# Deformable convolution on one Trainium2 core: transposes into shared PSUM banks, and a longer distance between transpose, copy and product

## The chip, the cores and the metric

The kernel runs on 1 core of one Trainium2 chip. A core has five engines that run side by side, each through its own list of instructions in order: TensorE (PE in the profile, with its weight loads as PEld), VectorE (DVE), ScalarE (ACT), GpSimd (POOL) and SyncE (SP, which only issues transfers here). Sixteen DMA engines move data between HBM and the on-chip memory SBUF. TensorE writes into PSUM, which has eight banks of 2 KB per partition. The metric is the device time of one execution in microseconds (us), median of five runs.

## The reference, cut to what matters

One layer of a vision model on `x` of shape (4, 256, 64, 64) in float32: a normalisation, a deformable 3x3 convolution, an attention over the images of the batch and a mixture of experts. The change lies in the convolution. For each pixel and each of the nine taps the reference predicts an offset and a mask, reads the image at the shifted place by bilinear interpolation (four corners, each with its own weight), and contracts the sampled values with the weights:

```python
off = om[:, :2 * K2].reshape(B, K2, 2, Ho, Wo)
mask = jax.nn.sigmoid(om[:, 2 * K2:])
...
ys = off[:, :, 0] + hs[None, None, :, None] + (ki * DIL)[None, :, None, None]
xs = off[:, :, 1] + ws[None, None, None, :] + (kj * DIL)[None, :, None, None]
sampled = jax.vmap(_bilinear)(x, ys, xs)
sampled = sampled * mask[:, None]
out = jnp.einsum('bckhw,ock->bohw', sampled, w_conv.reshape(O, C, K2))
```

## The kernel before, in words

**Steps.** The convolution is cut into 4 images x 288 = 1152 steps. A step `n` is one tap of one group of 128 pixels (`split`, L740 and on); four steps (`NT`) with the same tap make a block of 512 pixels, and nine taps make a finished block. Each step passes through the engines like this:

- `gather` (L746): POOL issues an indirect DMA that fetches 128 rows of 4 KB (the four corners of 128 pixels) from a table in HBM into one of ten buffers `g`. Gathers are issued in pairs, ten steps ahead, and each waits for the last corner of the step that used its buffer.
- `corner0` (L762): ACT multiplies the first corner by its weight into a tile `s`. It runs `LEAD` = 4 steps ahead.
- `corners` (L779): DVE adds the other three corners with three fused multiply-adds at L774: corner 1 of step n+2 into `partial`, corner 3 of step n+1 into its `s`, corner 2 of step n+2 into its `s`. After corner 3 the sample of a step is complete.
- `turned` (L784): PE transposes the two 128x128 halves of `s` into a PSUM tile `tps` (L788).
- `to_sbuf` (L792): ACT copies `tps` into a quarter of the tile `sT` of this tap (L796), `LAG` = 1 step later.
- `product` (L801): PE multiplies one of the four weight blocks of the tap with `sT`, 128x128 by 128x512, into an accumulator `acc` (L808), `TAP` = 5 steps after the sample. Each step has one such product.

**What else is in the same lists.** After nine taps a block is finished by `ended`: DVE adds the input image (`residual`, L819), PE transposes back and multiplies with the router (`by_token`, L828 and L834), ACT copies out (`done`, L843) and SP stores. Beside this, `pieces` prepares the next image: ACT normalises (L510), PE transposes it for the table (`turn`, L517), ACT copies (`leave`, L530), PE computes the offsets (`rows_of`, L548: six products of 512 columns per block of the image, a block of the image every `PERIOD` = 22 steps), ACT shifts them (L560), PE sums them (`summed`, L569), DVE takes them out (`kept`, L580) and makes positions and weights of them (L620 to L669). For the first image part of this runs during its own steps, and during the last image the first parts of the attention take its place (`first_blocks`).

**What sets the order.** For VectorE, ScalarE, TensorE and GpSimd the order is written out by hand: the loop over `n` calls the functions above in a fixed sequence, and each engine gets its instructions in the sequence of the calls. The waits between engines are put in by the framework from the tiles that are read and written. Two kinds of wait matter below. One is for data: `turned(n)` waits for corner 3 of step n, `to_sbuf` for the transposes, `product` for the copies. The other is for a buffer: `s` has `LEAD + 2` = 6 buffers, `sT` has 2, and the pool `ps_tp` has 3 PSUM banks, which `tps`, the table's transposes (L517) and the transposes back (L828) share.

**After the convolution** comes the attention and the mixture of experts, whose lists stand behind the last step of the convolution on every engine.

Of the kernel before, what the change touches and what calls it, by code (L numbers as in the profile page):

```python
# [9 lines left out]
F32 = mybir.dt.float32  # L10
# [7 lines left out]
P = 128  # L18
B, C, H, W = 4, 256, 64, 64
HW = H * W  # L20
NCH = C // P
K2 = 9
NR = HW // P
NOFF = 3 * K2
QUAD = 32
# [10 lines left out]
BLK = 512  # L36
NT = BLK // P
RB = BLK // W
# [2 lines left out]
STEPS = NR * K2  # L41
NGB = 10
AHEAD = NGB + 1
LEAD, LAG = 4, 1
TAP = LAG + NT
OUT = 6
EARLIEST = 12
FIRST = 32
# [54 lines left out]
def conv_attn_moe_kernel(  # L103
# [140 lines left out]
    state, qks, norms, tps, pending = {}, {}, {}, {}, []  # L244
# [88 lines left out]
    with ExitStack() as actx:  # L333
        aw = actx.enter_context(tc.tile_pool(name="a_w", bufs=1))
        ag = actx.enter_context(tc.tile_pool(name="a_gather", bufs=1))
        asm = actx.enter_context(tc.tile_pool(name="a_sm", bufs=5))
        ast = actx.enter_context(tc.tile_pool(name="a_stage", bufs=1))
        made = actx.enter_context(ExitStack())
        ap_ = actx.enter_context(tc.tile_pool(name="a_params", bufs=2))


        azt = made.enter_context(tc.tile_pool(name="a_zt", bufs=2, side="right"))
        apad = made.enter_context(tc.tile_pool(name="a_pad", bufs=2, side="right"))
        atmp = made.enter_context(tc.tile_pool(name="a_tmp", bufs=1, side="right"))
        axs = [
# [3 lines left out]
        ps_tp = actx.enter_context(tc.tile_pool(name="ps_tp", bufs=3, space=PSUM))  # L349
# [7 lines left out]
        def image_tile(b):  # L357
            xraw[b] = axs[b % 2].tile([P, NCH, HW], F32, name=f"xraw{b}", tag="xraw")
# [11 lines left out]
            load_piece(0, n)  # L370


        woff_sb = aw.tile([P, NCH, 3, 3, QUAD], F32, name="woff_sb")
        V.memset(woff_sb, 0.0)
        for ch in range(NCH):
            nc.sync.dma_start(
# [9 lines left out]
            V.tensor_copy(tap_sum[ps], ident[ps, kj * QUAD : kj * QUAD + NOFF])  # L386


        ocs = [aw.tile([3 * QUAD, RB, W], F32, name=f"oc{n}") for n in range(3)]
        for oc in ocs:  # L390
            V.memset(oc, 0.0)
        wconv_sb = aw.tile([P, NCH, K2, C], F32, name="wconv_sb")
# [2 lines left out]
        rwc_sb = load_router(aw, "rwc_sb")  # L395


        zeros = aw.tile([P, C], F32, name="zeros")
        G.memset(zeros, 0.0)

        def borders(b):
# [11 lines left out]
            )  # L413


        grid = aw.tile([P, 2, NR, K2], F32, name="grid")
        gi = atmp.tile([P, 2, NR, K2], I32, name="gi", tag="ki32")
        for half in range(2):
            ps = slice(half * 64, half * 64 + 64)
# [11 lines left out]
        def pieces(b):  # L431
# [31 lines left out]
            n = FIRST  # L463
# [20 lines left out]
            def block(q, at, table=True, offsets=True, alone=False):  # L484
# [66 lines left out]
                        start=(n == 0), stop=(n == NCH * 3 - 1),  # L551
                    )

                oc = ocs[q % 2 if table else 2]

                def shifted(kj):
                    ps = slice(kj * QUAD, (kj + 1) * QUAD)
# [180 lines left out]
        ss, tps, sTs, accs, sums, backs, outs, last_corner, gathers = ({} for _ in range(9))  # L738

        def split(n):  # L740
            b, m = divmod(n, STEPS)
            j, m = divmod(m, NT * K2)
            k, i = divmod(m, NT)
            return b, j * NT + i, k

        def gather(n):  # L746
            b, r, k = split(n)
            g = G.indirect_dma_start(  # L748
                out=gs[n % NGB], out_offset=None, in_=tables[b],
                in_offset=bass.IndirectOffsetOnAxis(  # L750
                    ap=params[b][0][:, r, k : k + 1], axis=0
                ),
            )


            buffer = f"buffer {n % NGB}"
            tc.declare_no_dep(g.ins, group=buffer, reason="ordered by the last corner")
            tc.add_to_no_dep_group(buffer, g.ins)
            gathers[n] = g
            return g  # L760

        def corner0(n):  # L762
            b, r, k = split(n)
            ss[n] = asm.tile([P, C], F32, name=f"s{n}", tag="s", bufs=LEAD + 2)
            first = S.activation(  # L765
                ss[n], gs[n % NGB][:, :C], AF.Copy, scale=params[b][1][:, 0, r, k : k + 1]
            )
            tc.add_to_no_dep_group(f"buffer {n % NGB}", first.ins)
# [10 lines left out]
        def corners(n):  # L779
            corner(n, 1)  # L780
            corner(n - 1, 3)
            corner(n, 2)

        def turned(n):  # L784
            s = ss.pop(n)
            tps[n] = ps_tp.tile([P, C], F32, name=f"tps{n}", tag="tp")
            for ch in range(NCH):
                T.transpose(  # L788
                    tps[n][:, ch * P : (ch + 1) * P], s[:, ch * P : (ch + 1) * P], ident
                )  # L790

        def to_sbuf(n):  # L792
            tap, i = divmod(n, NT)
            if i == 0:
                sTs[tap] = asm.tile([P, NCH, BLK], F32, name=f"sT{tap}", tag="sT", bufs=2)
            S.copy(  # L796
                sTs[tap][:, :, i * P : (i + 1) * P],
                tps.pop(n).rearrange("p (ch t) -> p ch t", ch=NCH),
            )
# [47 lines left out]
        def ended(block):  # L847

            m = (block * K2 + K2 - 1) * NT + TAP + NCH
            for oh in range(NCH):  # L850
# [14 lines left out]
        def put_off(n, fn):  # L865
            todo.setdefault(n, []).append(fn)
# [87 lines left out]
        with tc.manual_schedule(engines=order):  # L954
            total = B * STEPS
            for n in range(NGB):
                gather(n)
            for n in range(LEAD):
                corner0(n)
            for n in range(2):  # L960
                corners(n)
            for n in range(total + TAP + OUT + 3 * NT):
                b, at = divmod(n, STEPS)
                if at == LOADS[0] and b + 1 < B:
                    image_tile(b + 1)
                    for i, when in enumerate(LOADS):
                        put_off(b * STEPS + when, lambda b=b, i=i: load_later(b, i))
                    for when, fn in pieces(b + 1):
                        put_off(b * STEPS + when, fn)
                if n < total and n % (NT * K2) == 0:  # L970
                    ended(n // (NT * K2))
                if n + LEAD < total:
                    corner0(n + LEAD)
                if n + 1 < total:
                    corners(n + 2)
                if n < total:
                    turned(n)
                if LAG <= n < total + LAG:
                    to_sbuf(n - LAG)
                if 0 <= n - TAP < total:  # L980
                    product(n - TAP)
                if n == (B - 1) * STEPS + EARLIEST:
                    first_blocks()
                for fn in todo.pop(n, ()):
                    fn()

                if n % 2 == 0 and n + NGB < total:
                    g = gather(n + NGB)
                    tc.add_manual_dep(
                        g.ins, last_corner[n + 1].ins.name,  # L990
                        mybir.DependencyInfo(
                            mybir.DependencyClass.Sync, mybir.DependencyReason.DATA
                        ),
                        reason="the next gather's buffer",
                    )
                    gather(n + NGB + 1)
# [10 lines left out]
    for b in range(B):  # L1007
        for j in range(NBLK):
            if j < HB:
                n = j * B + b  # L1010
# [38 lines left out]
    with ExitStack() as bctx:  # L1049
# [4 lines left out]
        ps_tp = bctx.enter_context(tc.tile_pool(name="ps_tpb", bufs=3, space=PSUM))  # L1054
# [76 lines left out]
        total = len(blocks)  # L1131
# [130 lines left out]
    with ExitStack() as bctx:  # L1262
# [6 lines left out]
        ts, os_, pvs, pos_, lns, us, ss, bases = {}, {}, {}, {}, {}, {}, {}, {}  # L1269
# [589 lines left out]
    ps_tp = ctx.enter_context(tc.tile_pool(name="ps_tpm", bufs=2, space=PSUM))  # L1859
# [211 lines left out]
    with tc.manual_schedule(engines={nc.sync.engine, nc.gpsimd.engine}):  # L2071
        fixed.append(True)
        total = len(tiles)
# [79 lines left out]
```

## Time and profile before

| what | value |
|---|---|
| median of 5 runs | 2994.92 us (2992.09 to 3000.05) |
| the profiled execution's own time | 2991.32 us |
| its span in the profile | 2989.5 us |
| mean granted TensorE clock | 0.989 |
| PE busy | 2809.3 us, 94% of the span |
| DVE busy | 2459.3 us, 82% |
| ACT busy | 1897.8 us, 63% |
| POOL busy | 1759.1 us, 59% |
| moved by DMA | 913.00 MB, mean 305 GB/s |
| corners at L774, first and last start | 68.6 us and 1795.1 us |

The span of 2989.5 us is the time from the first to the last instruction that the profile shows; 1.8 us lie around it. The steps of the convolution take from 68.6 to 1795.1 us, 58% of the span, so 1152 steps take 1.50 us each. The page cuts the span into 40 slices of 74.7 us, and the convolution is about slices 2 to 24.

The page is read so: part 1 gives each engine's busy time, part 2 the busy share by slice in tenths, part 5 groups of equal instructions with their count, busy time, mean time of one, and the idle time of the engine just ahead of them with what ended it. A table by windows gives the busy time of each engine in a stretch of time, the granted clock and the DMA rate. A list of waits gives who waited for whom, in total us, times, and the longest.

Busy times of one group can overlap: an engine that works in a pipeline starts the next instruction before the last has ended. So an instruction's cost in a full stretch is the distance between starts, not its duration. In the timeline the products at L808 that follow each other without a break show 12 records in 5.32 us; one `product` of the kernel gives two records, one transpose gives one.

### The profile page before, as it was taken

To read this page: it belongs to the slowest core of one execution; us is meant where nothing else is said; L and a number is where in the kernel's file an instruction comes from. 1 tells how busy PE (TensorE), PEld (TensorE's weight loads), DVE (VectorE), ACT (ScalarE), POOL (GpSimd) and SP (SyncE) were. 2 spreads that over 40 slices of the span, in tenths; PEclk is the share of its full clock that TensorE was granted. 3 is DMA by queue.
4 is the path that set the end of the run, shared out by engine and by line. 5 is a ranking of instruction groups with operands and counts; after the bars stand their busy time and mean duration, and the time that the engine had idled before them with its cause. 6 is when DMAs were issued, how large, how long until landed. Compare 5 with 4: busy or idle time off the path is not lost. (4 is left out here: it accounts for less than half of the span.)

```text
span 2989.5 us, 45522 instructions
## 1 busy us (share of the span) xinstructions
PE 2809.3 (94%) x11356; PEld 1653.7 (55%) x11356; DVE 2459.3 (82%) x6413; ACT 1897.8 (63%) x4462; POOL 1759.1 (59%) x1809
## 2 busy tenths in 40 slices
PE   3899999899998899999999999999999999999997
PEld 2355554345554355544444444455555688888885
DVE  4988889998999999999999996988788785446777
ACT  2566665567765566765766664774876666666665
POOL 2665556666666666666777663320777677774442
PEclk8999999999999999999999999999999999999998
DMA  8999999999999999999999996961555656647988
GB/s 252 399 358 364 348 354 396 406 388 397 407 400 390 398 397 394 399 392 393 398 392 384 384 349 132 182 108 55 185 174 196 187 166 197 206 147 248 340 272 280
DMA packets 348547, 913.00 MB, mean 305 GB/s; under 512 B 42566, under 2 KB 125821, under 8 KB 345984
## 3 DMA queue, kind: packets, MB, share of 16 engines
q0 software_dynamic: 208368, 689.10, 62.5%
q1 hardware_dynamic: 129488, 197.93, 21.3%
q10 hardware_dynamic: 10432, 23.07, 2.0%
q8 instruction: 95, 1.56, 0.2%
q14 instruction: 164, 1.34, 0.1%
HBM read 741.09 MB, written 171.60 MB: 305 GB/s over the span
## 5 line engine op out<-in xcount | busy, mean ns | idle before, releaser
L748 POOL DMA_INDIRECT g<-table,idx x1152 | 1111.6, 965 | 626.8 <-DVE s L774 391.7
L808 PE MATMUL acc<-sT,wconv_sb 128*128 128x512 f32 x2304 | 1189.0, 598 | 29.9 <-ACT sT L796 28.0
L765 ACT ACTIVATE s<-g,wts 128x256 f32<-128x256 f32 x1152 | 586.4, 509 | 393.6 <-DMA g<-table,idx 305.2
L774 DVE SCALAR_TENSOR_TENSOR partial<-g,wts,s 128x256 f32<-128x256 f32 x1152 | 565.5, 491 | 131.6 <-ACT s L765 56.8
L788 PEld LDWEIGHTS tps<-ident,s 128*128 128x128 f32 x2304 | 296.4, 147 | 655.1 <-issue 271.7
L774 DVE SCALAR_TENSOR_TENSOR s<-g,wts,s 128x256 f32<-128x256 f32 x1152 | 551.2, 478 | 0.0
L774 DVE SCALAR_TENSOR_TENSOR s<-g,wts,partial 128x256 f32<-128x256 f32 x1152 | 546.8, 475 | 0.7
L788 PE MATMUL tps<-ident,s 128*128 128x128 f32 x2304 | 458.6, 281 | 85.0 <-DVE s L774 46.5
L796 ACT COPY sT<-tps 128x256 f32<-128x256 f32 x1152 | 414.5, 360 | 145.2 <-PE acc L808 80.9
L1935 POOL DMA_INDIRECT ys_rows<-y,to x277 | 275.1, 993 | 223.8 <-DVE y L1930 167.0
L808 PEld LDWEIGHTS acc<-sT,wconv_sb 128*128 128x128 f32 x2304 | 350.1, 192 | 42.3 <-ACT sT L796 39.3
L1508 POOL DMA_INDIRECT xs_rows<-u,slots x256 | 252.9, 988 | 92.7 <-issue 52.8
L1907 PE MATMUL ph<-xT,w 128*128 128x256 f32 (+1 forms) x1288 | 268.7, 352 | 7.0 <-ACT hT L1911 4.3
L1925 PE MATMUL py<-w,hT 128*128 128x256 f32 x1108 | 266.5, 380 | 0.6 <-ACT w L1874 0.6
L1930 DVE TENSOR_TENSOR y<-py,w 128x512 f32<-128x512 f32 (+1 forms) x161 | 99.4, 617 | 188.4 <-ACT w L1868 75.8
L1907 PEld LDWEIGHTS ph<-xT,w 128*128 128x128 f32 x1288 | 211.3, 191 | 28.0 <-ACT hT L1911 6.7
L1925 PEld LDWEIGHTS py<-w,hT 128*128 128x128 f32 x1108 | 207.4, 191 | 26.9 <-ACT w L1874 1.0
L1911 ACT ACTIVATE hT<-ph,w 128x256 f32<-128x256 f32 (+1 forms) x322 | 136.2, 442 | 128.2 <-PE ph L1907 126.5
L322 DVE SCALAR_TENSOR_TENSOR junk<-q,k 128x512 f32<-128x512 f32 x224 | 141.5, 687 | 20.4 <-ACT k L1107 20.3
L548 PE MATMUL po<-xs,woff_sb 128*96 128x512 f32 x288 | 147.3, 593 | 0.0
L1290 DVE SCALAR_TENSOR_TENSOR mix<-pv,att,mix 128x512 f32<-128x512 f32 x192 | 132.7, 743 | 6.8 <-PE pv L1026 2.8
L1874 ACT COPY w<-early_state 128x768 f32 x161 | 132.9, 825 | 0.0
(291 smaller groups left out, 3436.1 us busy)
## 6 DMA issues: line engine op xcount, KB each, us to landing
xt<-xs_rows SPq DMA_DIRECT2D x116, 260.0 KB
yk<-ys_rows SPq DMA_DIRECT2D x56, 512.0 KB
table<-zt SPq DMA_DIRECT2D x96, 256.0 KB
g<-table,idx POOLq DMA_INDIRECT x1152
t<-o SPq DMA_DIRECT2D x32, 530.0 KB
t<-bo_sb POOLq DMA_DIRECT2D x32, 530.0 KB
dt<-t SPq DMA_DIRECT2D x64, 265.0 KB
xraw<-in_x SPq DMA_DIRECT2D x16, 1024.0 KB
```

The source lines that it names most:

```text
L322: V.scalar_tensor_tensor(junk, qks[s_, j, ch][0], 1.0, qks[t_, j, ch][1], ALU.mult, ALU.mult, accum_out=parts[:, ch, s_ * B + t_, j : j + 1],)
L548: T.matmul(t["po"], woff_sb[:, ch, ki].rearrange("p kj o -> p (kj o)"), t["xs"][:, ch, ki : ki + RB], start=(n == 0), stop=(n == NCH * 3 - 1),
L748: g = G.indirect_dma_start(out=gs[n % NGB], out_offset=None, in_=tables[b], in_offset=bass.IndirectOffsetOnAxis(ap=params[b][0][:, r, k : ...
L765: first = S.activation(ss[n], gs[n % NGB][:, :C], AF.Copy, scale=params[b][1][:, 0, r, k : k + 1])
L774: last_corner[n] = V.scalar_tensor_tensor(kept if c == 1 else ss[n], gs[n % NGB][:, c * C : (c + 1) * C], params[b][1][:, c, r, k : k + 1] ...
L788: T.transpose(tps[n][:, ch * P : (ch + 1) * P], s[:, ch * P : (ch + 1) * P], ident)
L796: S.copy(sTs[tap][:, :, i * P : (i + 1) * P], tps.pop(n).rearrange("p (ch t) -> p ch t", ch=NCH),)
L808: T.matmul(accs[block, oh], wconv_sb[:, ch, k, oh * P : (oh + 1) * P], sTs[tap][:, ch, :], start=(k == 0 and ch == 0), stop=(k == K2 - 1 a ...
L1508: s = G.indirect_dma_start(out=rows_, out_offset=bass.IndirectOffsetOnAxis(ap=slots[:, k, n : n + 1], axis=0), in_=u[:, n % NT, :], in_off ...
L1907: T.matmul(ph, w1_sb[:, ch, f * P : (f + 1) * P], xT[:, ch, :], start=(ch == 0), stop=(ch == NCH - 1),)
L1925: T.matmul(py[:, i, :], hT[:, f, i * P : (i + 1) * P], w2_sb[:, f, :], start=(f == 0), stop=(f == NCH - 1),)
L1935: s = G.indirect_dma_start(out=ys_rows[g], out_offset=bass.IndirectOffsetOnAxis(ap=to[:, i : i + 1], axis=0), in_=y[:, i, :], in_offset=No ...
```

## The change

Four things change in the convolution.

1. **Pairs in PSUM.** `turned` makes a tile of two steps (2 KB per partition, a full bank) at every even step, and the odd step writes the second half. The pool still has 3 banks.
2. **Distances.** PE transposes step n-1 instead of n (`TURN` = 1), ACT copies step n-3 instead of n-1 (`LAG` = 3), and the product stands 9 steps behind the sample instead of 5 (`TAP` = `LAG + NT + 2`). All that hangs on `TAP` (adding the input, transposing back, storing) moves 4 steps later with it.
3. **More buffers.** `s` gets `LEAD + TURN + 2` = 7 instead of 6, `sT` 3 instead of 2.
4. **Room for them.** The offset weights, the grid, the zeros and the tiles `oc` move into a pool that is given back when the last table has been made, and `oc` has two tiles instead of three: one for the tables of later images instead of two in turn, one for the first image.

The number of instructions of each kind and engine stays the same, but for one memset of `oc` less on DVE. Behind the convolution the lists of PE, ACT and DVE are the same in both kernels. On SP a store of a finished block changes places with a border store once, and with two weight loads once; on POOL one memset moves ahead of some constants.

```diff
-LEAD, LAG = 4, 1
-TAP = LAG + NT
+LEAD, TURN, LAG = 4, 1, 3
+TAP = LAG + NT + 2
...
+        amade = made.enter_context(tc.tile_pool(name="a_made", bufs=1, side="right"))
...
-        woff_sb = aw.tile([P, NCH, 3, 3, QUAD], F32, name="woff_sb")
+        woff_sb = amade.tile([P, NCH, 3, 3, QUAD], F32, name="woff_sb")
...
-        ocs = [aw.tile([3 * QUAD, RB, W], F32, name=f"oc{n}") for n in range(3)]
+        ocs = [amade.tile([3 * QUAD, RB, W], F32, name=f"oc{n}") for n in range(2)]
...
-                oc = ocs[q % 2 if table else 2]
+                oc = ocs[0 if table else 1]
...
-            ss[n] = asm.tile([P, C], F32, name=f"s{n}", tag="s", bufs=LEAD + 2)
+            ss[n] = asm.tile([P, C], F32, name=f"s{n}", tag="s", bufs=LEAD + TURN + 2)
...
         def turned(n):
             s = ss.pop(n)
-            tps[n] = ps_tp.tile([P, C], F32, name=f"tps{n}", tag="tp")
+            if n % 2 == 0:
+                pair = ps_tp.tile([P, 2, C], F32, name=f"tps{n}", tag="tp")
+                tps.update({n: pair[:, 0, :], n + 1: pair[:, 1, :]})
             for ch in range(NCH):
                 T.transpose(
                     tps[n][:, ch * P : (ch + 1) * P], s[:, ch * P : (ch + 1) * P], ident
...
-                sTs[tap] = asm.tile([P, NCH, BLK], F32, name=f"sT{tap}", tag="sT", bufs=2)
+                sTs[tap] = asm.tile([P, NCH, BLK], F32, name=f"sT{tap}", tag="sT", bufs=3)
...
-                if n < total:
-                    turned(n)
+                if TURN <= n < total + TURN:
+                    turned(n - TURN)
                 if LAG <= n < total + LAG:
                     to_sbuf(n - LAG)
                 if 0 <= n - TAP < total:
                     product(n - TAP)
```

More of the change, by code (lines that the diff above doesn't have):

```diff
@@ L395, in conv_attn_moe_kernel @@
         rwc_sb = load_router(aw, "rwc_sb")
-        zeros = aw.tile([P, C], F32, name="zeros")
+        zeros = amade.tile([P, C], F32, name="zeros")
         G.memset(zeros, 0.0)
@@ L413, in borders @@
             )
-        grid = aw.tile([P, 2, NR, K2], F32, name="grid")
+        grid = amade.tile([P, 2, NR, K2], F32, name="grid")
         gi = atmp.tile([P, 2, NR, K2], I32, name="gi", tag="ki32")
```

## The prediction

> **What bounds the kernel now.** First the busy shares by slice on the page, to find the stage and its engines:
>
> ```profile
> PE   3899999899998899999999999999999999999997
> ...
> DVE  4988889998999999999999996988788785446777
> ACT  2566665567765566765766664774876666666665
> ...
> DMA  8999999999999999999999996961555656647988
> ```
>
> In the slices of the convolution (2 to 24) PE, DVE and DMA all stand at 8 or 9 and ACT at 6: the slices alone don't say who sets the pace. So I asked for the table by windows of 100 us from 80 to 1780 us (PE, PEld, DVE, ACT, POOL busy, then clock, DMA share, GB/s):
>
> ```profile
> 280.00:380.00 100.00, 98.62 (x380) 51.12 (x379) 82.43 (x216) 66.68 (x161) 56.20 (x61) 1.00 0.98 358
> ...
> 680.00:780.00 100.00, 100.00 (x411) 54.33 (x410) 89.54 (x212) 71.70 (x176) 64.44 (x70) 1.00 1.02 399
> 780.00:880.00 100.00, 100.00 (x414) 54.58 (x414) 91.65 (x228) 69.96 (x175) 64.59 (x70) 1.00 1.03 403
> 880.00:980.00 100.00, 90.52 (x329) 42.53 (x328) 91.90 (x216) 55.11 (x146) 65.28 (x70) 0.97 1.01 393
> 980.00:1080.00 100.00, 89.06 (x322) 40.63 (x322) 96.36 (x239) 58.40 (x148) 65.60 (x68) 1.00 1.01 392
> ```
>
> The stage has two kinds of stretch. Where the next image's table and offsets are made (180 to 480, 680 to 880, 1080 to 1280: the seven P windows) PE is full: its seven busy times are 98.46, 98.62, 97.15, 100, 100, 99.06 and 99.78, so it idles 6.9 us in 700. In the other ten, the D windows, PE has 4 to 13 us free in each and DVE sets the pace. DVE's idle there is 62.3 us in 1000, but most is not waiting. In the timeline corner 1 starts 0.57 us after corner 2, which took 0.48, with no releaser named: a fixed distance that the change does not touch:
>
> ```profile
> 1791.82 0.47 DVE L774 SCALAR_TENSOR_TENSOR s<-g,wts,partial 128x256 f32<-128x256 f32 x1
> 1792.39 0.49 DVE L774 SCALAR_TENSOR_TENSOR partial<-g,wts,s 128x256 f32<-128x256 f32 x1
> ```
>
> So I asked for the waits of DVE alone. In the D windows they are 3.1 us (80 to 180), 3.8 (480 to 680), 3.5 (880 to 1080), 5.4 (1280 to 1480) and 1.2 (1480 to 1780): 17.0 us in all. In one of these windows, 880 to 1080, the waits of all engines show what is behind them:
>
> ```profile
> ACT s L765 <- DMA g<-table,idx: 56.2, 79, 2.7
> ...
> ACT sT L796 <- PE acc L808: 6.1, 9, 1.4
> ...
> DVE partial L774 <- ACT s L765: 3.5, 8, 0.8
> ```
>
> The reader is to see that DVE waits for corner 0, and that ACT, which makes it, is mostly held by gathers, little by PE.
>
> **What this says of the ceiling.** The page shows large waits, but a wait counts only on the engine that is full in its stretch. DVE waits 55 us in the P windows (21.9 us of it on PE's sums at L569), yet PE could not have gone faster there by more than 6.9 us. PE waits for DVE's corner 3 in the D windows, where DVE is the bound. If every wait on the full engine went, the stage would gain 6.9 + 17.0 = 23.9 us of 2991.
>
> **The change part by part.**
>
> *Transposes one step behind.* `turned` no longer needs the corner 3 that DVE has just finished. In the P windows this is PE's wait of 2.5 us (180 to 480, L788 on DVE s; none is shown in the other four P windows). It goes. PE may also enter each P stretch up to one step ahead. A step's PE work is two transposes and a product; in the timeline transposes to product is 0.22 us and a product 0.86 (the 12 records between 1796.10 and 1801.25 us are six products), so 1.08. Three P stretches give 0 to 3.2 us; PE is held by ACT's copies as well as by DVE, so I take 2.
>
> *Products four steps further behind, third `sT`.* The wait of products for copies (L808 on ACT sT, 2.1 us in 180 to 480) goes; with the 2.5 that is 4.6 of the 6.9 us, and I take 4.6 (bounds 0 and 6.9). ACT's wait for a free `sT` (L796 on PE acc, 80.9 us on the whole page) should nearly vanish, since the third buffer gives it three steps of room instead of one. ACT is 60 to 70% busy, so this pays only where it made corner 0 late. I went back from each of the 17.0 us in the D windows to what had held ACT: about 9 us end at a gather that had not landed, which the change cannot hurry. Bounds 0 and 17.0; I take 7, nearer to 17.0 - 9.
>
> *Pairs.* The transposes of a step, their copies and their PSUM space cost the same instructions as before. Two waits are new. The copy of an even step now waits for the odd step's transposes too, as they share a bank; behind it on ACT stands the next corner 0, and DVE waits for that. The copies stand one step behind those transposes, as every copy did before, when a copy started 1.3 us (P) to 1.8 us (D) after its transposes in the middle case: hidden. And the waits written into the built program show that the transposes of an even step, where a table is made, wait for the copy of three steps before, which stands one step earlier on ACT (elsewhere five steps before); the table's transposes take turns in the same three banks. Before, every step waited for the copy of two or three steps before, also one step earlier on ACT. So half of these waits go and the other half keeps its distance. I take 0 for it; the rival below prices it.
>
> *The tail.* After the last corner 3, PE has nine products to go instead of six, and the attention's list stands behind them on PE. Three more products cost 3 x 0.86 = 2.6 us:
>
> ```profile
> 1795.88 0.38 PE L788 MATMUL tps<-ident,s 128*128 128x128 f32 x2
> 1796.10 5.32 PE L808 MATMUL acc<-sT,wconv_sb 128*128 128x512 f32 x12
> 1801.25 0.27 PE L828 MATMUL back<-ident,sum 128*128 128x128 f32 x1
> ```
>
> PE is at 100% soon behind it (1816 to 1846 us), so this is on the path. At the start the later products cost nothing: PE is 88% busy from 80 to 180 us.
>
> *Moved tiles, one `oc`, order on SP.* One `oc` for the tables is written again 17 steps (25 us) after its last sums; if that cover were gone, a wait like DVE's longest on L569, 3.4 us, could come once per block. A store that changes places with two weight loads on SP is read no sooner than before; 0, at worst one landing of some 8 us as for the stores at the end of the chain. The memset of `oc` that goes (0.54 us) lies before the first image has landed: 0.
>
> **A rule that speaks against it.** The rate of DMA in the windows above goes up to 403 GB/s, in a slice of the page to 407, at a share of 1.0. The Trainium skill (DMA: Bandwidth & Descriptors, Where 436 GB/s comes from) says that about 358 GB/s binds for transfers between HBM and SBUF and 435 GB/s is the ceiling of the fabric. The first figure would make any gain here impossible; the rows already stand above it. By the second, an estimate, the stage's 390 GB/s would leave some 10%, more than the change can use. Likewise the skill (PSUM — Partial Sum Buffer, PSUM bank collisions raise a hardware error) asks that two engines be kept apart by bank, not by address, which agrees with the wait of the even copy on the odd transposes; no row of before shows such a pair.
>
> **Sum.** 4.6 + 2 + 7 - 2.6 = 11.0 us less. The profiled execution took 2991.3 us (span 2989.5 and 1.8 around it), so 2980.3 on its own scale. It lies 3.6 us under the median of the five, 2994.9; on the median's scale the forecast is 2983.9, taken as 2984.
>
> **Rivals.**
>
> *Nothing is left (0.27).* All 17.0 us of the D windows turn out to be the gathers', and the P windows gain 4.6 at most: 4.6 - 2.6 = 2 us, 2993. For it: 56.2 us against 6.1 in the waits of ACT above, and a DMA share of 1.0.
>
> *Larger (0.15).* PE's busy time is modelled, so a window of 98% may hide stalls. If half of DVE's 55 us of waits in the P windows also go with the new room: 11 + 27 = 38 us, or with only a third 29; I price it at 2960. Against it: the starts of products there keep to 0.43 us a record.
>
> *Slower (0.13).* In the P windows PE is full, so any new wait on it shows in the time. The place is the transposes of even steps, held by the copy three steps before, which in turn stands behind corner 0 and its gather on ACT. 700 us at 1.50 us a step are 467 steps, 233 pairs. In 680 to 880 us PE's weight loads waited on such copies 24 times for 6.5 us, 0.27 each, all hidden behind the matmul before. If a third of the pairs wait that long in the open: 78 x 0.27 = 21, and the tail 2.6: 24 us, 3018. It decides from the point where ACT's copy ends after PE has finished the product before it; in the P windows the copy of two steps before ended 1.5 us ahead of the transposes in the middle case, and after them in 7 cases of 100, so ACT would have to lose about a step.
>
> **Numbers.** 0.45 for the forecast (2977 to 2989), 0.27 for nothing left, 0.15 for larger, 0.13 for slower. About 0.2%, 6 us, is what a measurement of this kernel can tell from no change, so faster is 0.45 + 0.15 = 0.60, same 0.27, slower 0.13. The range reaches from 2962 (all 23.9 us, the 3.2 of the lead, and some of the larger case) to 3002 (nothing left and the lower part of the slower case).
>
> **What would show it.** Right: in the P windows PE stays at 98 to 100% and the windows only get shorter by 1%; ACT's wait at L796 for acc falls from 80.9 us to under 20; the D windows' waits of DVE fall from 17 to about 10, all behind gathers; nine products at the end. Wrong: PE's share falling under 97% in the P windows with the transposes (L791 there) waiting for copies (slower), or DVE's om waits gone and PE showing more work per us (larger).

## The result, and the profile after

The changed kernel takes **2999.81 us** (median, 2993.51 to 3006.11). The kernel before, run beside it, takes 2993.85: ratio 1.0019, 95% interval [1.0014, 1.0024]. The interval lies wholly above 1, so it is slower, by about the 0.2% (6 us) that the prediction took for the least that can be told; the forecast was 2984 and faster. The span of the profiled execution is 2994.4 us against 2989.5, at the same mean clock of 0.989. Beside the runs e9 to e18 the kernel before itself took 3336 to 3379 us, at a mean clock of 0.94; those runs are compared only with each other.

The busy shares by slice of the changed kernel:

```profile
PE   4899998899998899998999999999999999999997
...
DVE  4988889998998998999999996887788785445777
ACT  2566765566665566655676664665876666666675
...
DMA  8999999999999999999999996961555656657988
```

PE, DVE and DMA stand at 8 or 9 in the convolution as they did, and nothing in this view tells the kernels apart. The table by windows (PE, PEld, DVE, ACT, POOL busy with counts, then clock, DMA share, GB/s):

```profile
280.00:380.00 100.00, 100.00 (x395) 52.97 (x393) 82.35 (x219) 67.16 (x163) 56.35 (x61) 1.00 0.96 354
680.00:780.00 100.00, 98.91 (x405) 53.55 (x404) 88.82 (x211) 68.30 (x170) 64.28 (x68) 1.00 1.02 394
780.00:880.00 100.00, 100.00 (x407) 53.84 (x406) 92.08 (x228) 69.27 (x175) 64.68 (x69) 1.00 1.02 399
880.00:980.00 100.00, 88.93 (x334) 41.49 (x333) 89.91 (x213) 55.00 (x146) 65.21 (x69) 1.00 1.01 394
980.00:1080.00 100.00, 86.59 (x325) 41.21 (x325) 96.01 (x238) 58.51 (x150) 66.70 (x67) 1.00 1.01 390
```

The reader is to look at the counts. From 680 to 880 us PE is still "full" at 98.91 and 100.00, but it starts 405 + 407 matmul records there, before 411 + 414. A record of a product lasts 0.59 us while the next starts after 0.43, so busy time says "full" well before the engine is. In 280 to 380 us, in image 0, the count rises from 380 to 395. A single window also shifts with where its edges cut the steps, so the table by groups of steps further down is the safer measure. The waits from 880 to 1080 us:

```profile
ACT s L766 <- DMA g<-table,idx: 55.1, 85, 2.4
...
PE tps L791 <- ACT sT L799: 15.1, 19, 1.8
DVE partial L775 <- ACT s L766: 6.3, 16, 1.1
```

ACT's wait for products (6.1 us before) has gone from the list; its wait for gathers has not moved (56.2 to 55.1), and DVE waits longer for corner 0 (3.5 to 6.3), not less. The end of the convolution, DVE's last corners and then PE:

```profile
1795.97 0.47 DVE L775 SCALAR_TENSOR_TENSOR s<-g,wts,partial 128x256 f32<-128x256 f32 x1
1796.53 0.49 DVE L775 SCALAR_TENSOR_TENSOR partial<-g,wts,s 128x256 f32<-128x256 f32 x1
```

```profile
1798.66 0.38 PE L791 MATMUL tps<-ident,s 128*128 128x128 f32 x2
1798.88 7.89 PE L811 MATMUL acc<-sT,wconv_sb 128*128 128x512 f32 x18
1806.61 0.27 PE L831 MATMUL back<-ident,sum 128*128 128x128 f32 x1
```

The corners keep their distance of 0.56 us, and 18 records, nine products, take 7.89 us where 12 took 5.32. From the last corner 1 to the start of the last record it is 9.7 us, before 7.1: 2.6 us of tail. The rest of the loss is in the steps, and small: the last corner 1 starts at 1796.5 instead of 1793.7.

**Where the waits of ACT went.** ACT's waits from 68 to 1796 us, before:

```profile
ACT s L765 <- DMA g<-table,idx: 305.2, 457, 14.3
ACT sT L796 <- PE acc L808: 80.9, 123, 2.9
ACT sT L796 <- PE tps L788: 60.3, 113, 1.6
ACT s L765 <- DVE s L774: 52.6, 85, 2.5
...
ACT zt L530 <- PE tpx L517: 37.9, 59, 1.6
```

and after:

```profile
ACT s L766 <- DMA g<-table,idx: 318.1, 467, 13.1
ACT zt L531 <- PE tpx L518: 85.5, 68, 2.8
ACT s L766 <- DVE s L775: 67.7, 99, 3.0
...
ACT sT L799 <- PE tps L791: 35.4, 64, 2.0
ACT s L766 <- DVE partial L775: 26.1, 44, 2.1
ACT s L766 <- PE tps L791: 24.7, 42, 1.5
```

The 80.9 us are gone and 25 us of the wait for transposes with them. The same time comes back in front of the next instruction that can't go on: the table's transposes (37.9 to 85.5), gathers (305.2 to 318.1), buffers `s` (52.6 to 67.7, and 24.7 for transposes that still read them, which the list of before does not have). All of ACT's waits in this stretch together are 620 us before and 637 after. DVE's wait for corner 0 over all steps is 56.8 and 57.5 us.

**A new wait.** With the products `residual` moves four steps back, and the load of the next image's first quarter writes the buffer that `residual` reads. SP's waits from 68 to 1796 us, first before, then after:

```profile
SPq L363 <- DVE s L774: 221.3, 12, 35.4
```

```profile
SPq L364 <- DVE s L775: 133.2, 10, 19.6
...
SPq L364 <- DVE sum L822: 70.3, 2, 35.3
```

Twelve loads waited only for their place in the order; now two of them, the first of images 2 and 3, wait for the sum of the block before and start at step 10.1 of the image instead of 6.7. DVE's statistics of the image then wait for data that had always been there (1.1 us in all).

Time by groups of steps, from the starts of corner 1, in us (D: no table is made, P: a table is made):

| steps | before | changed | e2 | e5 | e6 | e7 | e8 |
|---|---|---|---|---|---|---|---|
| 0-60, D | 97.5 | 97.4 | 96.8 | 95.9 | 96.2 | 96.8 | 96.7 |
| 60-250, P, image 0 | 307.4 | 305.8 | 307.4 | 307.4 | 305.8 | 279.2 | 279.3 |
| 250-348, D | 146.5 | 148.3 | 146.2 | 144.1 | 144.5 | 146.5 | 149.1 |
| 348-538, P, image 1 | 277.6 | 279.0 | 279.0 | 277.1 | 274.2 | 274.5 | 274.9 |
| 538-636, D | 147.3 | 148.7 | 146.1 | 143.9 | 144.1 | 147.8 | 148.2 |
| 636-826, P, image 2 | 282.8 | 282.8 | 283.1 | 280.7 | 277.7 | 277.5 | 278.2 |
| 826-924, D | 138.7 | 138.9 | 137.3 | 136.6 | 136.8 | 138.3 | 138.1 |
| 924-1151, D | 327.5 | 327.0 | 326.6 | 327.1 | 327.0 | 328.9 | 327.0 |

e2 is before with the third `sT` alone, e5 and e6 are before and changed with gathers of half the size, e7 and e8 before and changed with five of six offset products left out. Each column is one execution, so a single cell is worth a microsecond or two; the P group of image 0 repeats better than that (307.4 in before, e2 and e5, 305.8 in the changed kernel and e6).

DVE's own waits in the D groups behind step 60, added up in the same way, say more than the windows of 100 us, which cut into P groups: 11.0 us before, 14.4 in the changed kernel, 7.4 in e2, 0.9 in e5 and 2.2 in e6.

### The profile page after: what moved, and what is told of

Same layout as the page of the kernel before. It is cut to its first block, busy times and chain, and to the rows that moved or that the text cites. A ratio compares the mean times of both kernels' runs of the same rounds, so it can differ in the third digit from the quotient of the medians.

```text
span 2994.4 us, 45056 instructions
## 1 busy us (share of the span) xinstructions
PE 2805.6 (94%) x11356; PEld 1655.5 (55%) x11356; DVE 2459.3 (82%) x6412; ACT 1884.7 (63%) x4462; POOL 1761.1 (59%) x1809
## 5 line engine op out<-in xcount | busy, mean ns | idle before, releaser
L766 ACT ACTIVATE s<-g,wts 128x256 f32<-128x256 f32 x1152 | 586.0, 509 | 454.4 <-DMA g<-table,idx 318.1
L775 DVE SCALAR_TENSOR_TENSOR partial<-g,wts,s 128x256 f32<-128x256 f32 x1152 | 565.6, 491 | 131.1 <-ACT s L766 57.5
L799 ACT COPY sT<-tps 128x256 f32<-128x256 f32 x1152 | 411.2, 357 | 39.2 <-PE tps L791 37.7
L549 PE MATMUL po<-xs,woff_sb 128*96 128x512 f32 x288 | 147.3, 593 | 0.0
```

Source lines behind the costliest of these rows:

```text
L549: T.matmul(t["po"], woff_sb[:, ch, ki].rearrange("p kj o -> p (kj o)"), t["xs"][:, ch, ki : ki + RB], start=(n == 0), stop=(n == NCH * 3 - 1),
L766: first = S.activation(ss[n], gs[n % NGB][:, :C], AF.Copy, scale=params[b][1][:, 0, r, k : k + 1])
L775: last_corner[n] = V.scalar_tensor_tensor(kept if c == 1 else ss[n], gs[n % NGB][:, c * C : (c + 1) * C], params[b][1][:, c, r, k : k + 1] ...
L799: S.copy(sTs[tap][:, :, i * P : (i + 1) * P], tps.pop(n).rearrange("p (ch t) -> p ch t", ch=NCH),)
```

## The experiments

**First, the terms of the prediction one by one.** My theory after the result: three limits, PE, DVE and the gathers, lie so close that room on one of them is taken up by the next; the tail and the late load then decide. Rival: the new layout itself costs waits (pairs in three banks, copies behind corner 0) that cancel a real gain.

*e1: the changed kernel with a product two steps nearer.*

```diff
-TAP = LAG + NT + 2
+TAP = LAG + NT
```

> The changed kernel with the product 7 steps behind the sample instead of 9, all else as changed. Theory A (the full engine of each stretch sets the time; the change only moved waits and lengthened the tail): seven products instead of nine behind the last transposes, 2 x 0.86 = 1.7 us less than the changed kernel, about 1.0013 of before. Rival B (the room between copies and products is worth something): slower than the changed kernel, above 1.0019. Rival C (shared PUSM banks of the pairs hold PE): no difference to the changed kernel, 1.0019.

3000.4 us, ratio 1.0023, [1.0010, 1.0035]. The tail is 8.4 us (9.7 in the changed kernel, 7.1 before), so 1.2 of the expected 1.7 us came back at the end, but not in the time, which can't be told from the changed kernel's 1.0019: the two later P groups took 280.8 and 284.7 us, 1.8 and 1.9 more than in the changed kernel. PE's waits from 68 to 1803 us show what the shorter distance costs inside:

```profile
PE acc L811 <- ACT sT L799: 73.9, 69, 3.5
```

In the changed kernel no wait of a product for a copy is in the list, and before they came to 28.0 us. PE stops 25 times for over 1.5 us during the steps of e1 (7 times in the changed kernel, 5 before), and the granted clock is 0.50 for 37.5 us of them (3.4 in the changed kernel). So the two steps of room between copy and product do remove waits of PE; what that is worth in time can't be told here.

*e2: the third `sT` alone.* Distances and single tiles as before, with the moved pool.

```diff
-LEAD, TURN, LAG = 4, 1, 3
-TAP = LAG + NT + 2
+LEAD, TURN, LAG = 4, 0, 1
+TAP = LAG + NT
```

> The distances and single PSUM tiles of before, with the changed kernel's pool layout and three sT buffers: of the change, only the third sT and the moved tiles are left. Theory A: the wait of copies for a free sT (80.9 us on ACT) falls under 20, and the time stays within 3 us of before (0.999 to 1.001). Rival B (ACT's waits for PE made corner 0 late and so cost time): 6 us or more faster, below 0.998. If the new layout itself costs something, it shows here as above 1.001.

2992.17 us, 0.9996 [0.9987, 1.0006]: no change. ACT's waits from 68 to 1796 us:

```profile
ACT s L766 <- DMA g<-table,idx: 291.5, 469, 2.9
ACT sT L797 <- PE tps L789: 106.3, 169, 2.0
```

The wait of 80.9 us for a free `sT` is gone, and 46 us of it stand one line further, at the transposes (60.3 before). This is the cheapest form of what happened to the whole change: most of ACT's wait moved on by one line. It is not all of it. DVE's waits in the D groups behind step 60 fall from 11.0 to 7.4 us, and these groups are 3.7 us shorter together, while the P groups are 1.7 longer. All steps together are 2.7 us shorter in this one execution, and the medians' 2.1 us lie inside the interval of no change.

*e3: the copies of the table and of the finished blocks later on ACT* (changed kernel), so that they no longer hold it up.

```diff
-                        out_.append((at + 4 + 4 * i, lambda i=i: leave(i)))
+                        out_.append((at + 6 + 4 * i, lambda i=i: leave(i)))
...
-                put_off(m + OUT + 2 * i + 1, lambda i=i: done(block, i))
+                put_off(m + OUT + 2 * i + 2, lambda i=i: done(block, i))
```

> The changed kernel, with the copies of the table's transposes two steps later (three behind them instead of one) and those of the transposes back one step later. Theory A: ACT's waits there (85.5 and 58.7 us in the changed kernel) fall under 60 together, and the time falls by 0 to 5 us against the changed kernel (1.0003 to 1.0019 of before), as PE is full where tables are made. Rival B (these two waits took the place of the ones removed and ate a gain of some 14 us): 10 us or more faster than the changed kernel, below 0.9985 of before.

3007.59 us, 1.0040 [1.0027, 1.0053], some 6 to 8 us worse than the changed kernel, which neither theory had foreseen. ACT's two waits leave its list, but its wait for transposes at L799 rises from 35.4 to 128.0 us. PE's waits from 68 to 1803 us:

```profile
...
PE tps L791 <- ACT sT L799: 38.0, 57, 1.7
PE acc L811 <- DVE sum L822: 13.6, 27, 0.9
PE back L831 <- ACT o L846: 11.7, 15, 2.1
PE back L831 <- ACT sT L799: 11.6, 12, 1.7
```

A later copy holds its bank of the pool of three longer, and PE waits for banks at the transposes back: `back` on copies of `o`, 11.7 us, is not among PE's waits of the changed kernel. That this is what costs the time is argued: a fourth bank would test it, and the convolution's pools take all eight (3 + 1 + 2 + 2).

*e4: the kernel before with the table's work spread wider.*

```diff
-PERIOD = 22
+PERIOD = 25
-BORDERS = 236
+BORDERS = 257
```

> The kernel before with one block of the next image's table every 25 steps instead of 22 (and the borders' store at step 257 instead of 236): the same work on PE spread over more steps, no distance or buffer changed. Theory A (PE is full where tables are made, and DVE elsewhere): a period's PE work of 22 x 1.535 = 33.8 us takes 37.5 us with three more steps of 1.25, where before it took 33.8 and three steps of 1.475, 38.2; 0.7 us for 24 blocks, about 17 us, at least 8: 0.994 to 0.997 of before. Rival B (short waits between the engines cost the time, not a full PE): no gain, 0.999 or above.

2993.43 us, 0.9998 [0.9990, 1.0007]. The P groups got shorter (277.6 to 273.8, 282.8 to 275.5 us) and the D groups behind them longer (147.3 to 153.0, 138.7 to 143.6). So 8 us or more for a PE that is full, as theory A had it, did not come. The run doesn't settle it alone: the first gathers of images 1 and 2 start 2.8 and 6.2 us late (0.5 before), probably behind the later store of the borders.

**Then one limit taken away at a time.**

*e5 and e6: half the bytes of each gather,* on the kernel before and on the changed one. The right-hand corners are not fetched and count as zeros or old values; two of the ten buffers are cleared first.

```diff
-                out=gs[n % NGB], out_offset=None, in_=tables[b],
+                out=gs[n % NGB][:, : 2 * C], out_offset=None, in_=tables[b],
```

> The kernel before with gathers of 2 KB a row instead of 4: the two right-hand corners are not fetched, DVE still adds what stands in the buffers. Every instruction of PE, DVE and ACT stays. Theory A (PE full where tables are made, DVE elsewhere, gathers hold the rest): DVE's waits behind gathers go, and what is left is the full engines: 10 to 30 us faster, 0.990 to 0.997. Theory D (the gathers' rate sets the time over each image, so that what one stretch gains another loses): 25 us or more faster, below 0.992. Rival B (short waits between PE and ACT): under 6 us, above 0.998.

> The changed kernel with the same half gathers. Theory A: the change still buys nothing, 0 to 6 us slower than the kernel before with half gathers (the tail of 2.6 us and what moved waits cost). Theory D: with the gathers out of the way the new room pays: 6 us or more faster than the kernel before with half gathers.

Before: 2979.37 us, 0.9948 [0.9934, 0.9962]. Changed: 2976.98, 0.9935 [0.9921, 0.9948]. ACT's waits in e5, 68 to 1796 us:

```profile
ACT sT L798 <- PE acc L810: 254.7, 251, 3.6
ACT sT L798 <- PE tps L790: 186.9, 327, 2.0
...
ACT s L767 <- DMA g<-table,idx: 29.2, 38, 3.1
```

and in e6:

```profile
ACT s L768 <- DMA g<-table,idx: 148.2, 209, 4.0
```

With lighter gathers ACT's waits on them fall from 305.2 to 29.2 us. In the table by steps the D groups up to 924 lose 9.5 us (the sum of 1.6, 2.4, 3.4 and 2.1): that is close to the "about 9 us that end at a gather" of the prediction, and DVE's waits in the D groups behind step 60 all but go (11.0 to 0.9). The P group of image 0 stays at 307.4 us, so there the gathers hold nothing. And now the change pays where it was meant to: e6 is 2.9 and 3.0 us faster than e5 in the P groups of images 1 and 2, and 1.6 in that of image 0. With full gathers those two groups gained -1.4 and 0.0. Over all steps it is 6.4 us faster in e6 than in e5, in the medians 2.4: the tail of 2.6 us stays, and in the trace the steps of e6 start 1.0 us later. The two intervals overlap, and 2.4 us faster is neither the 0 to 6 us slower of theory A nor the 6 us or more of theory D, so the sum is weaker evidence than its place.

*e7 and e8: five of six offset products left out,* on both kernels, so that PE has far less to do in the P groups. Offsets and addresses come out different.

```diff
-                        start=(n == 0), stop=(n == NCH * 3 - 1),
+                        start=True, stop=True,
...
-                    for m in range(NCH * 3):
+                    for m in range(1):
```

> The kernel before with one of the six products that make the offsets of a block, five left out (160 products of 0.86 us, so PE has some 130 us less to do, nearly all where tables are made; offsets and addresses are other ones). Theory A: the P windows take the step of the D windows, 1.475 instead of 1.535 us: 27 us faster, at least 15, 0.988 to 0.995. Theory D: the gathers hold the P stretches as well; under 12 us, above 0.996.

> The changed kernel with the same five of six offset products left out. Theory A: no better than the kernel before with them left out, 0 to 6 us slower. Rival B (the new room pays where PE is not full): 6 us or more faster than it.

Before: 2959.87 us, 0.9881 [0.9866, 0.9896]; changed: 2963.24, 0.9896 [0.9880, 0.9911]. The windows of e7, behind the first of them in the kernel before:

```profile
180.00:280.00 100.00, 98.46 (x403) 53.21 (x402) 83.61 (x223) 70.46 (x168) 57.70 (x61) 1.00 0.96 353
...
180.00:280.00 100.00, 93.85 (x395) 50.27 (x394) 94.28 (x248) 74.55 (x182) 66.04 (x70) 1.00 1.03 401
680.00:780.00 100.00, 93.16 (x374) 49.07 (x374) 90.46 (x216) 70.53 (x175) 66.74 (x70) 0.98 1.03 409
```

In image 0 the P group falls from 307.4 to 279.2 us: there PE was the limit (DMA moved 353 GB/s in that window before, 401 now). In images 1 and 2 the same relief gives 3.1 and 5.3 us of 280, though PE drops to 93% busy. So behind PE, at 1 to 2%, stands another limit; the gathers, at a DMA share of 1.03, fit it best after e6, and DVE, 90% busy, may have a part. "PE is full, hence PE sets the pace" was true for one P stretch in three. The time meets theory A's range at its edge (0.9881), but 28 of the 36 us come from image 0, not from all P groups. The other offsets also send the gathers to other rows of the table; what that alone does wasn't tried. With PE off the path the change costs 3.4 us in the medians (in the traces 2.6 of tail and 2.2 in the steps).

**Then the parts, to find which one loses the 2.8 us in the steps.** e9 loads the images and starts their pieces four steps later; e10 has the transposes a step behind, without pairs; e11 the pairs, without that; both with copies two steps behind and the product six. e12 is e4 with a smaller spread.

```diff
 e9, on the changed kernel
-FIRST = 32
-LOADS = (8, 18, 28, 38)
+FIRST = 36
+LOADS = (12, 22, 32, 42)
 e10, on the changed kernel, with single tiles in turned
-LEAD, TURN, LAG = 4, 1, 3
-TAP = LAG + NT + 2
+LEAD, TURN, LAG = 4, 1, 2
+TAP = LAG + NT
 e11, on the changed kernel
-LEAD, TURN, LAG = 4, 1, 3
-TAP = LAG + NT + 2
+LEAD, TURN, LAG = 4, 0, 2
+TAP = LAG + NT
 e12, on the kernel before
-PERIOD = 22
+PERIOD = 24
-BORDERS = 236
+BORDERS = 242
```

> The changed kernel with the next image's four loads 4 steps later (steps 12, 22, 32, 42 instead of 8, 18, 28, 38) and what follows them in step (FIRST 36 instead of 32). Theory E (the change moved the last use of the image's buffer behind the step of the first load, so the load comes 3.4 steps late and crowds the next one and the gathers): DVE's wait for the image (1.1 us) goes and the two stretches around the image's start shorten by 2 to 4 us together: 1.0004 to 1.0014 of before. Rival: the late load costs nothing, 1.0019 as the changed kernel.

> Of the change only the transposes one step later (TURN 1, copies at 2, products at 6, so copy and product keep their distances to the transposes), with three sT and seven s; single PSUM tiles as before. Six products behind the last transposes as before, so no longer tail, and the image's buffer is free in time. Theory A: no room that the full engine can use, 0.9993 to 1.0007. Rival B (DVE's corner 3 held PE): 6 us or more faster, below 0.998.

> Of the change only the pairs in PSUM (transposes in their own step, copies at 2, products at 6), with three sT. One product more behind the last transposes, 0.9 us. Theory C (pairs and the table's transposes take turns in three banks, and PE waits for copies): 2 to 8 us slower than before, 1.0007 to 1.0027, with PE's wait for copies above the 17 us of before. Without C: 1.0003.

> The kernel before with a block of the next image's table every 24 steps and the borders' store at step 242, right behind the last table store. With 25 steps and the borders at 257 the two P stretches of images 1 and 2 were 3.8 and 7.3 us shorter, and the first gathers of images 1 and 2 waited 2.8 and 6.2 us. If those waits were the late borders': 2 to 8 us faster than before, 0.9973 to 0.9993. If the gathers' rate takes back what PE gains (theory D): 0.9995 to 1.0005.

The kernel before took 3379.05 us beside these four. e9 3366.68, 0.9967 [0.9949, 0.9985]; e10 3357.62, 0.9939 [0.9917, 0.9961]; e11 3351.5, 0.992 [0.9891, 0.9949]; e12 3378.68, 0.9998 [0.9975, 1.0022]. Parts of a change that gains nothing now gain 0.3 to 0.8%. So the parts were run again, with the changed kernel itself beside them:

> The changed kernel with the image loads and the first piece of each image four steps later, so that no load waits for an addition that has not been made. The time before here is near 2995 if the chip grants its full clock. If the late load is what costs the 1.8 and 1.4 us of the steps 250 to 348 and 538 to 636: 3.2 us less than the changed kernel, ratio about 1.0008. If that cost comes from the longer room itself (another order of waits on ACT): within 1 us of the changed kernel, 1.0015 to 1.0020.

> Transposes one step behind, copies one step behind those, product at the old six-product distance plus one, single tiles instead of pairs. If the transposes' step is what gains and the pairs lose: 0.9975 to 0.999. If there is nothing to gain because table, gathers and VectorE limit within 1 to 2 per cent of each other: 0.9995 to 1.0015, the tail costing at most 1.7 us.

> Pairs in PSUM with the transposes at their old place, copies two steps behind, one step more for the product. If pairs relieve PE of waits for copies: 0.997 to 0.999. If pairs in three banks cost waits: 1.001 to 1.003. If nothing is left to gain: 0.9995 to 1.0015.

> The changed kernel itself, on the same chip as the other three, as the point they are compared with. At full clock 1.0019 as before. On a chip that grants a lower clock, where PE is the longer engine: 0.992 to 0.998, as its parts did there.

Before 3375.12; e13 (as e9) 3369.72, 0.9982 [0.9962, 1.0003]; e14 (as e10) 3354.56, 0.9933 [0.9908, 0.9959]; e15 (as e11) 3350.65, 0.9926 [0.9899, 0.9952]; e16, the changed kernel, 3352.59, 0.9926 [0.9899, 0.9952]. And a third time for two of them:

> The changed kernel with image loads and first pieces four steps later, a third try to see it where the clock is full (before near 2995). There: 1.0008 if the late load costs the 3.2 us by which the steps 250 to 348 and 538 to 636 are longer, 1.0015 to 1.0020 if it doesn't. Where the clock is 0.94 (before near 3375): 0.997 to 0.998 as in the two runs before, which says that starting the pieces later costs more there than the load's wait.

> Pairs with the transposes at their old place, copies two steps behind, seven products at the end. At full clock: 0.9990 to 1.0000 if the step's delay of the transposes and the longer tail are what made the changed kernel slower, 1.001 to 1.003 if the pairs themselves cost. At a clock of 0.94: 0.992 to 0.993 as before.

Before 3336.07; e17 3316.66, 0.9935 [0.9914, 0.9956]; e18 3311.85, 0.9923 [0.9897, 0.9950].

The changed kernel, 0.2% slower than a kernel before of 2994 us, is 0.7% (22.5 us) faster than one of 3375. The chip alone does not make that difference: on the one of e17 and e18 the kernel before took 2995.56 us beside e5 to e8. What the parts were to show, where the 2.8 us of the steps go at 2994, none of these runs shows. Of the expectations for the lower clock, those of e16 and e18 came in, and e17's (0.997 to 0.998) did not. A trace shows what these executions have besides a lower clock. ACT's row of instructions in e16:

```profile
522.51 0.36 ACT L799 COPY sT<-tps 128x256 f32<-128x256 f32 x1
529.79 0.38 ACT L846 COPY o<-back 128x265 f32<-128x265 f32 x1 [6.92 <-remote]
530.07 0.51 ACT L766 ACTIVATE s<-g,wts 128x256 f32<-128x256 f32 x1
```

and the windows just behind it:

```profile
530.00:532.00 2.00, 1.78 (x9) 1.78 (x10) 1.30 (x4) 1.90 (x7) 0.00 (x0) 0.50 0.95 383
532.00:534.00 2.00, 2.00 (x5) 0.86 (x5) 1.91 (x5) 1.32 (x4) 0.88 (x1) 0.50 0.66 269
```

ACT stands still for 6.92 us, with "remote" as the releaser, which is none that the trace can name; the product of PE that it copies had ended at 522.3. PE and DVE run dry behind it, and when PE returns its clock is 0.50 for some five microseconds. From 80 to 1950 us there are 43 PE gaps over 1.5 us in e16 and 50 in e12, which has the old distances; the trace of the kernel before at 2991 us has 5. Why the change gains among such stops is not shown: turn alone, pairs alone and the whole change agree within their intervals. What the three share is the third `sT`, copies at least a step further behind and a later product. Starting the pieces later takes some of the gain away again beside e16 (e13, the intervals lie apart), but not beside e18 (e17).

## Why the prediction was wrong

- **The tail, +2.6 us: right**, to the tenth (7.1 to 9.7 us). Behind it the rest of the kernel takes 1188.3 us in the changed trace and 1188.7 before, so nothing absorbed it.
- **Transposes and products in the P windows, -4.6 and -2: failed.** The step was "In the P windows PE is full, so a PE wait removed is time". The P groups together went from 867.8 to 867.6 us. In image 0 PE is the limit (e7: 28.2 us) and 1.6 us came. In images 1 and 2 the gathers are a limit as well: with full gathers the change brings -1.4 and 0.0 us there, and a gain of 2.9 and 3.0 only when they are halved (e5 to e6), one execution each. I had read a busy share of 100 as a limit on its own, with a DMA share of 1.02 to 1.03 in the same rows.
- **DVE's waits in the D windows, -7: failed.** They went from 17.0 to 20.4 us. The step was to take what is left of 17.0 beside the 9 us of the gathers as the missing `sT` buffer's. In the D groups themselves, behind step 60, DVE waits only 11.0 us, and with half gathers 0.9 are left (e5): nearly all of it is the gathers'. ACT's 80.9 us at `acc` did fall to 0, as forecast, and turned up in front of other instructions (e2 shows it for the buffer alone: 60.3 to 106.3 us at the transposes, time 0.9996). The buffer alone may be worth half of the 7 (e2: 7.4 us of waits, D groups 3.7 us shorter); with the distances, the pairs and the late load on top these waits are 14.4, so those three together put 7.0 us back. These are sums over one execution each, and they overlap: a late corner 0 can have both a gather and a buffer behind it. Which of the three costs what is open.
- **The step that was not in the sum: `residual` moves with `TAP`.** I costed the later products only at the start and the end. The first image load now waits for it; the D groups 250 to 348 and 538 to 636 are 1.8 and 1.4 us longer, 1.5 and 1.9 in e3, and -0.3 and -1.2 in e2, where the load is in its old place. The D group 826 to 924, which has no load, is 0.3 us longer in the changed kernel and as before in e3. That the load is the cause is still argued: DVE's direct wait for it is only 1.1 us; the same late load goes with 0.4 and 0.2 us under halved gathers (e6 against e5) and with 2.6 and 0.4 under less PE work (e8 against e7); in e1, where it starts 1.4 steps late instead of 3.4, the two groups are 3.1 and 1.2 us longer, but many of that run's PE stops lie in them; and e9, e13 and e17, which were to show it, ran beside a kernel before of 3336 to 3379 us.
- **The rivals.** "Nothing is left" named the cause (the gathers) and gave 2993; the result is 7 us above it mostly because that case let the P windows gain 4.6 us and left the D groups as they were, which are 3 us longer. "Slower" had the wrong place: from 680 to 880 us PE's only wait in the list is 1.1 us, and its waits for copies (17.3 to 44.4 us over all steps) lie mostly where PE has room, as in the 15.1 us above. One of its signs did show: PE's share fell under 97% in two P windows (96.62 at 380 us, 96.60 at 1080 us), but the transposes wait for copies only 2.2 and 1.4 us in those stretches. "Larger" found nothing: DVE's waits in the P windows are 55.1 us before and 55.0 after.
- **Sum of the steps:** -13.6 forecast, +2.8 measured. The tail made it +5.4 in the trace (span +4.9), and 6.0 in the medians. The stated range reached up to 3002, but by waits of PE for banks that are not what happened, so that it holds 2999.8 is luck.
- **Two small readings** were off, without weight in the sum: DVE's waits on PE's sums at L569 in the P windows are 22.4 us, not 21.9, and PE's free time in the D windows is 3 to 13 us, not 4 to 13.

On the rate of transfers, DMA: Bandwidth & Descriptors (Where 436 GB/s comes from) of the Trainium skill was weighed in the prediction by its ceiling of 435 GB/s, which left 10% of room. None of the windows of 100 us shown here goes above 409 GB/s (e7), even with PE relieved, so the room that these runs show over the stage's 390 is 5%, half of that estimate; the lower figure of that page, 358, is passed in most of these windows.

Left open: which part of the change costs the steps' 2.8 us, since the parts e9, e10 and e11 never ran beside a kernel before of 2994 us; and what stops ACT in e16.

## What to carry to other kernels

A wait that disappears from one line of a list is a gain only if the next thing the engine needs is ready; before counting it, ask what that next thing is, and whether every other engine and queue in the same window has more than a few per cent left. A busy share near 100 beside a full DMA share can mean two limits, and removing a wait on one of them then gives at most the difference between the two, not the wait: here PE alone held the stretch with a DMA share of 0.96 to 0.99 (28.2 us when relieved), and not the two with 1.02 to 1.03 (3.1 and 5.3 us). When a distance grows, list everything that hangs on it, the buffer releases too: here a load in another part of the kernel moved with the products.

## What the runs showed of the hardware

- From 180 to 280 us, in image 0, transfers reach 401 GB/s when PE has less to do (e7), against 353 in the same window of the kernel before. From 680 to 780 us the same relief brings only 399 to 409.
- A PE gap of 2.1 us at 911.7 us in the kernel before was followed by a clock of 0.50 from 913 to 920 us, while one of 2.57 us at 552.5 us in the changed kernel was followed by none.
- With 25 PE stops of 1.6 to 4.3 us in the steps of e1 the clock was 0.50 for 37.5 us there; the changed kernel, with the same work, had 7 stops and 3.4 us.
- In e16 ACT stopped for up to 7.6 us with no releaser that the trace names, and PE had 43 gaps over 1.5 us. The kernel before took 11 to 13% longer beside e9 to e18; an estimate from the clocks, if all of the time followed them, gives 5% (0.989 over 0.942 is 1.05), so the lower clock is at most about half of it.
